# Probabilities and values in 32 bits in a banded attention and feed-forward kernel, with another order of issue

## The chip, the cores and the metric

The kernel runs on one core of one Trainium2 chip. The metric is the device time of one execution in microseconds (us); the time of a kernel is the median of its runs. A core has five engines that run side by side and meet at semaphores: TensorE (PE, whose weight loads are a row of their own, PEld), VectorE (DVE), ScalarE (ACT), GpSimd (POOL) and SyncE (SP, which issues the transfers). Each engine takes its instructions in the order in which the program lists them.

## What is computed

One layer of a transformer in 32 bit floats over 4 sequences of 2048 rows of 256: layer norm, attention in 16 heads of 16 in which each row sees itself and the 63 rows before it, a residual sum, layer norm, a feed-forward block with weights rounded to -1, 0 and 1, and a residual sum.

```python
x = x + attention(layernorm(x), Wq, Wk, Wv, Wo)
x = x + ffn(layernorm(x), W1, b1, W2, b2)

# attention
scores = einsum('bhqd,bhkd->bhqk', q, k) / sqrt(16) + bias   # bias: 0 where i-64 < j <= i, else -inf
attn = softmax(scores, axis=-1)
out = einsum('bhqk,bhkd->bhqd', attn, v)
return einsum('bsd,ed->bse', out.reshape(B, S, D), Wo)

# ffn
h = relu(einsum('bsd,fd->bsf', x, ternary(W1)) + b1)
return einsum('bsf,df->bsd', h, ternary(W2)) + b2
```

## The kernel before

The 8192 rows are cut into 32 chunks `c` of 256 rows, and a chunk into 4 blocks `b` of 64 query rows. A block of queries meets a window of 128 keys. TensorE multiplies 16 bit operands, so the kernel writes each 32 bit operand as a high and a low 16 bit part and adds two or three products of parts.

A chunk goes through these steps. `norm_in` normalises and splits the rows and transposes them by a transfer into `xT`. `project` makes q, k and v; for v (L627) the product in PSUM is cast into the high half of a tile `vo` by ACT (L643), the rest is subtracted into its low half by DVE (L645), and three transfers (L649, L651, L655) copy the rows into `ve`, the same values shifted by 64 rows, so that blocks of even number also find their window in one tile. A column of ones beside each pair's 32 value columns makes the sum of the probabilities fall out of the same product. `stack` puts parts of q and k over each other into `st`, so that one product does the work of three. `maxima` (L731) multiplies queries and keys for the row maximum, which DVE takes (L738) and a transfer writes back into `st`. `weights` (L771) multiplies again, now with the maximum subtracted inside the product, into a PSUM bank of 128 keys by 512 columns (8 heads of 64 queries, in two halves `g` per block).

The two steps that the change touches come next. `weights` takes the exponential of that bank and splits it. In the variant used for all 256 half blocks, ACT writes the exponential in 32 bits to a tile `r` (L781), casts it to the 16 bit `ph` (L784), and POOL subtracts to get `pl` (L786). `values` multiplies: for each of the 8 pairs of heads in a block, three products accumulate in one PSUM place, high by high (L812), high by the low part of the values (L813) and low by high (L814). In each, the probabilities, 128 keys by 128 queries of the two heads, are loaded into TensorE's array as weights, and 34 or 32 value columns are streamed past. DVE then takes the reciprocal of the sums (L827) and scales (L830) into `o`.

`wo_out` (L861) projects the result, `normalized` normalises it, and `ffn1` (L896) and `ffn2` (L936, L937) are the feed-forward block. `ffn1` also has two variants to split its result: ACT writes the high part (L915) and DVE subtracts (L917), or ACT writes 32 bits (L906), casts (L909) and POOL subtracts (L911).

The order of all this is not the order of the source. Each step is a generator that yields the engine it is about to use and a planned cost (`"P", 0.6` for a block of `values`). The class `Lanes` runs a plan with these costs: of the steps that could start soonest it takes the one with the lowest priority number, which is made from the chunk, `PRIO`, `SLOPE` and `EARLY`. What it takes is issued then, and `chain` ties each engine's instructions in that order. `Lanes.pick` chooses between the variants of a step by the load that the plan has put on each engine, weighted with `WT`. So a change of a planned cost or of these tables moves instructions of every kind, and can send a step to another engine. Rings of buffers (`BUFS`) limit how far steps run ahead: 6 PSUM banks in all, of which `values` holds at most 4 (`pv`), and 6 tiles or pairs of tiles of probabilities (`pp`).

Of the kernel before, what the change touches and what calls it, by code (L numbers as in the profile page):

```python
# [10 lines left out]
FP = mybir.dt.float32  # L11
HP = mybir.dt.float16
BF = mybir.dt.bfloat16
U8 = mybir.dt.uint8
AF = mybir.ActivationFunctionType
ALU = mybir.AluOpType
# [20 lines left out]
PARTS = slice(64, 112)  # L37
R = 113
BIGH = 60000.0
PRIO = {'norm': 22.87, 'proj': 45.21, 'max': -15.41, 'att': 28.99, 'val': -103.79, 'wo': -72.86, 'ffn': -195.42, 'ffn2': 67.42, 'mask': 69.79, 'prep': -8.89}  # L40
SLOPE = {'norm': 0.0, 'proj': 0.051, 'max': 0.158, 'att': 0.043, 'val': 0.156, 'wo': 0.0, 'ffn': -0.016, 'ffn2': 0.0, 'mask': 0.106, 'prep': -0.017}
BUFS = {'xt': 11, 'ln': 2, 'xT': 3, 'zT': 4, 'qk': 2, 'pp': 6, 'op': 2, 'o': 2, 'h': 7, 'r': 5, 'bank': 6, 'lin': 6, 'sp': 1, 'tp': 3, 'pv': 4}
BANKS = ("lin", "tp", "pv")
EARLY = {'norm': (0.0, 0.0, -1.01), 'proj': (0.0, 6.69, -1.97), 'max': (0.0, 0.0, 0.0), 'att': (0.0, -2.82, 0.0), 'val': (0.0, 6.48, 0.0), 'wo': (0.0, 0.0, -1.66), 'ffn': (0.0, 0.0, 0.0), 'ffn2': (0.69, 0.0, -3.29), 'mask': (0.0, 0.0, 0.0), 'prep': (0.0, -20.19, 0.0)}
TOL = 0.0
BOOST = 4.14
CHAIN = ('PE', 'DVE', 'Activation', 'Pool', 'SP')
LAT = {"P": 0.2, "A": 0.17, "D": 0.15, "G": 0.13, "S": 0.97}
TAU = 17.1
DMAF, DLAT = 1.06, 0.78  # L50
WINDOW = 3.4133
WT = {'P': 0.82, 'A': 1.13, 'D': 1.02, 'G': 0.94, 'S': 0.0}


class Lanes:
# [147 lines left out]
def kernel(ctx: ExitStack, tc: tile.TileContext, x, Wq, Wk, Wv, Wo, W1, b1, W2, b2, out):  # L203
# [32 lines left out]
    def get(name):  # L236
        return ("get", name)
# [37 lines left out]
    qcon = const.tile([128, C], HP, name="qcon")  # L275
    qone = const.tile([1, C], HP, name="qone")

    vot = [const.tile([128, 2, NT, NP, 34], HP, name=f"vo{i}") for i in range(NV)]
    vet = [const.tile([128, 2, NT, NP, 34], HP, name=f"ve{i}") for i in range(NV)]

    xts, xTs, vs, ps_, hs, wts = {}, {}, {}, {}, {}, {}

# [2 lines left out]
    def constants():  # L285
        yield "G", 0.4
        make_identity(nc, ident)
        yield "D", 0.605
        nc.vector.memset(mhalf, -0.5)
        nc.vector.memset(ones, 1.0)  # L290
        nc.vector.memset(shift, PSHIFT * 4.0)
        signal("const")
        yield "D", 0.3
        nc.vector.tensor_copy(identh, ident)
        signal("ident")
        for i in range(NV):
            yield "G", 0.9
            nc.gpsimd.memset(vot[i][:, :, :, :, 32:34], 0.0)
            nc.gpsimd.memset(vot[i][:, 0, :, :, 32:33], 1.0)
            nc.gpsimd.memset(vet[i][0:64, :, 0], 0.0)  # L300
            nc.gpsimd.memset(mht[i % NQ], 0.0)
            signal("vfree", i - NV)

# [35 lines left out]
    def loaded(src, key):  # L339
        yield get("xt")  # L340
        yield "S", (0.5, 0.9)
        wn = xpool.tile([128, 2, D], FP, name="xt")
        nc.sync.dma_start(out=wn, in_=src)
        wts[key] = wn
        signal("loaded", key)
# [266 lines left out]
    def project(c, nm):  # L612
        yield wait("weight", nm)
        yield wait("normed", c)
        xT = xTs[c]
        wh, wl = wts[nm]
        if nm == "v":
            yield wait("vfree", c - NV)
        yield get("lin")
        yield "P", 1.32  # L620
        ps = lin.tile([128, 2, C], FP, name="bank")
        if nm == "v":
            for t in range(NT):
                n = 0
                for d in range(2):
                    for i, b in ((0, wh), (1, wh), (0, wl)):
                        nc.tensor.matmul(ps[:, t, :], xT[:, i, d, t, :], b[:, d, :], start=n == 0, stop=n == 5)  # L627
                        n += 1
        else:
            for e in range(2):  # L630
                es = slice(e * 128, (e + 1) * 128)
                n = 0
                for d in range(2):
                    for a, i in ((wh, 0), (wh, 1), (wl, 0)):
                        nc.tensor.matmul(ps[:, e, :], a[:, d, es], xT[:, i, d], start=n == 0, stop=n == 5)  # L635
                        n += 1
        if tally(("proj", c), 3):
            put("xT")
        if nm == "v":
            vo, ve = vs[c] = vot[c % NV], vet[c % NV]  # L640
            psv = ps.rearrange("p u (a r) -> p u a r", r=32)
            yield "A", 0.485
            nc.scalar.copy(vo[:, 0, :, :, 0:32], psv)  # L643
            yield "D", 0.605
            nc.vector.tensor_tensor(vo[:, 1, :, :, 0:32], psv, vo[:, 0, :, :, 0:32], ALU.subtract)  # L645
            put("lin")
            signal("vo", c)
            yield "S", (0.6, 0.75)
            nc.sync.dma_start(out=ve[64:128], in_=vo[0:64])  # L649
            yield "S", (0.72, 0.4)  # L650
            nc.sync.dma_start(out=ve[0:64, :, 1:NT], in_=vo[64:128, :, 0:NT - 1])  # L651
            if c % NCB:
                yield wait("vo", c - 1)
                yield "S", (0.72, 0.4)
                nc.sync.dma_start(out=ve[0:64, :, 0], in_=vs[c - 1][0][64:128, :, NT - 1])  # L655
                if tally(("vdone", c - 1), 2):
                    signal("vfree", c - 1)
            if (c + 1) % NCB == 0 and tally(("vdone", c), 2):
                signal("vfree", c)
            signal("v", c)  # L660
            return
        if ("hl", c) not in ps_:
            ps_["hl", c] = None
            yield get("qk")
            ps_["hl", c] = qkp.tile([128, 2, 2, 2, C], HP, name="hl")
            signal("hl", c)
        yield wait("hl", c)
        hl = ps_["hl", c][:, "qk".index(nm)]
        yield "A", 0.485
        nc.scalar.copy(hl[:, 0], ps)  # L670
        yield "D", 0.605
        nc.vector.tensor_tensor(hl[:, 1], ps, hl[:, 0], ALU.subtract)
        put("lin")
        signal(nm, c)
# [88 lines left out]
    def weights(c, b, g):  # L763
        yield get("pp")
        yield get("tp")
        yield "P", 0.24
        tp = tps.tile([128, 8, W], FP, name="bank")
        for i in range(8):
            j = g * 8 + i
            h = place(j)  # L770
            nc.tensor.matmul(tp[:, i], window(c, h, b)[0:R + 1], st[c % NQ][0:R + 1, 0, h, b * W:b * W + W], start=True, stop=True)  # L771
        used(c)
        tpf = tp.rearrange("p h q -> p (h q)")
        ph = pp.tile([128, 4, 128], HP, name="ph")
        pl = pp.tile([128, 4, 128], HP, name="pl")
        phf, plf = (t.rearrange("p a b -> p (a b)") for t in (ph, pl))
        if lanes.pick([[("D", 0.605), ("A", 0.97)], [("G", 1.2), ("A", 1.005)]]):
            yield get("r")
            yield "A", 0.485
            pf = rp.tile([128, 512], FP, name="r")  # L780
            nc.scalar.activation(pf, tpf, AF.Exp, scale=0.25 / (SW * SW))  # L781
            put("tp")
            yield "A", 0.52
            nc.scalar.copy(phf, pf)  # L784
            yield "G", 1.2
            nc.gpsimd.tensor_tensor(plf, pf, phf, ALU.subtract)  # L786
            put("r")
        else:
            yield "A", 0.485
            nc.scalar.activation(tpf, tpf, AF.Exp, scale=0.25 / (SW * SW))  # L790
            yield "A", 0.485
            nc.scalar.copy(phf, tpf)
            yield "D", 0.605
            nc.vector.tensor_tensor(plf, tpf, phf, ALU.subtract)
            put("tp")
        ps_[c, b, g] = (ph, pl)
        signal("p", c, b, g)

    def values(c, b):
# [3 lines left out]
        vo, ve = vs[c]  # L803
        v = vo if b % 2 else ve
        yield get("pv")
        yield "P", 0.6
        pv = pvp.tile([128, NP, 34], FP, name="bank")
        for g in range(2):
            ph, pl = ps_.pop((c, b, g))
            for i in range(4):  # L810
                p = g * 4 + i
                nc.tensor.matmul(pv[:, p, :], ph[:, i, :], v[:, 0, b // 2, p, :], start=True, stop=False)  # L812
                nc.tensor.matmul(pv[:, p, 0:32], ph[:, i, :], v[:, 1, b // 2, p, 0:32], start=False, stop=False)  # L813
                nc.tensor.matmul(pv[:, p, :], pl[:, i, :], v[:, 0, b // 2, p, :], start=False, stop=True)  # L814
            put("pp")
        if tally(("val", c), NB) and tally(("vdone", c), 2):
            signal("vfree", c)
# [128 lines left out]
        put("xt")  # L946

    for i, gen in enumerate([constants(), load(0)]):
        lanes.add(-9 + i, gen)
    for i, (nm, src) in enumerate((("q", Wq), ("k", Wk), ("v", Wv))):  # L950
        lanes.add(-7 + i, loaded(src.rearrange("(c p) d -> p c d", p=128), nm))
        start("proj", 0, weight_qkv(nm), i - 5)
    for c in range(NCH):
        if c:
# [34 lines left out]
```

## Time and profile before

| | |
|---|---|
| median of 3 runs | 671.49 us (671.26 to 676.62) |
| the profiled execution | 671.55 us |
| span of its instructions on the core | 669.8 us |
| mean granted TensorE clock | 0.987 |
| PE busy | 93% |
| DVE, ACT, POOL busy | 83%, 79%, 83% |

The profile gives each engine's busy time, cuts the span into 40 slices with the busy share of each in tenths, follows back the chain that ended last, and lists the costliest groups of instructions: line, engine, operation, tile written and tiles read with their shapes, the count, then the busy time and the mean of one in ns, then the engine's idle time ahead of them and who ended it. A matmul's record runs from its start until its modelled end, and records of successive matmuls overlap: a group of 1024 matmuls of 177 ns does not fill 1024 x 177 ns. What a matmul costs the engine is read from the distance between the starts of successive records in the timeline.

### The profile page before, as it was taken

To read this page: it belongs to the slowest core of one execution; us is meant where nothing else is said; L and a number is where in the kernel's file an instruction comes from. 1 tells how busy PE (TensorE), PEld (TensorE's weight loads), DVE (VectorE), ACT (ScalarE), POOL (GpSimd) and SP (SyncE) were. 2 spreads that over 40 slices of the span, in tenths; PEclk is the share of its full clock that TensorE was granted. 3 is DMA by queue.
4 is the path that set the end of the run, shared out by engine and by line. 5 is a ranking of instruction groups with operands and counts; after the bars stand their busy time and mean duration, and the time that the engine had idled before them with its cause. 6 is when DMAs were issued, how large, how long until landed. Compare 5 with 4: busy or idle time off the path is not lost.

```text
span 669.8 us, 30496 instructions
## 1 busy us (share of the span) xinstructions
PE 626.2 (93%) x12892; PEld 548.3 (82%) x12892; DVE 556.4 (83%) x1195; ACT 529.1 (79%) x1074; POOL 558.5 (83%) x639
## 2 busy tenths in 40 slices
PE   2867889999999999999999999999999999999997
PEld 1646777888888888888888879898788888988986
DVE  6788989888987998898989898878878997897763
ACT  6966969877999689988879969686879589987741
POOL 5676989979899879998989979898789689998830
PEclk9977998999999999999999999999999999999999
DMA  6684465766777668865785665589555954542232
GB/s 180 167 154 107 82 130 115 120 129 109 138 132 127 133 115 132 146 115 142 143 140 127 131 96 141 119 142 145 90 124 126 156 122 106 116 107 60 49 81 62
DMA packets 165032, 81.34 MB, mean 121 GB/s; under 512 B 110880, under 2 KB 162848, under 8 KB 164896
## 3 DMA queue, kind: packets, MB, share of 16 engines
q1 hardware_dynamic: 164896, 79.39, 61.5%
q8 instruction: 101, 1.65, 1.2%
q14 instruction: 35, 0.29, 0.2%
HBM read 11.67 MB, written 8.39 MB: 30 GB/s over the span
## 4 chain that ended last, share of the span: by engine, by line
PE 56%; POOL 13%; DVE 11%; ACT 7%; DMA 6%; issue 5%; SPq 3%; POOLq 0%; DVEq 0%; ACTq 0%
PE bank L896 11%; PE bank L635 7%; POOL pl L786 7%; PE bank L771 6%; PE bank L936 6%; PE bank L937 5%; PE sp L731 5%; PE bank L861 5%; PE bank L627 3%; DMA xt<-in_dram 3%; PE bank L814 3%; PE bank L812 2%; PE bank L813 2%; DVE mx L738 2%; ACT ph L784 2%
## 5 line engine op out<-in xcount | busy, mean ns | idle before, releaser
L786 POOL TENSOR_TENSOR pl<-r,ph 128x512 f16<-128x512 f32 x256 | 304.5, 1210 | 17.3 <-ACT ph L784 10.9
L781 ACT ACTIVATE r<-bank 128x512 f32<-128x512 f32 x256 | 145.5, 599 | 32.2 <-PE bank L771 26.9
L784 ACT CAST ph<-r 128x512 f16<-128x512 f32 x256 | 151.0, 629 | 0.7
L738 DVE TENSOR_REDUCE mx<-sp 128x8 f32<-128x768 f32 x128 | 121.8, 952 | 14.7 <-PE sp L731 13.0
L896 PE MATMUL bank<-zT,wq 128*128 128x256 f16 x1024 | 125.5, 273 | 0.3 <-DVE hl L917 0.2
L936 PE MATMUL bank<-wq,hh 128*128 128x256 f16 x512 | 119.7, 273 | 0.0
L937 PE MATMUL bank<-wq,hl 128*128 128x256 f16 x512 | 119.2, 272 | 0.0
L917 DVE SCALAR_TENSOR_TENSOR hl<-bank,hh 128x512 f16<-128x512 f32 x126 | 85.2, 685 | 34.8 <-ACT hh L915 33.2
L896 PEld LDWEIGHTS <-wq 128*128 128x128 f16 x1024 | 97.8, 98 | 12.5 <-issue 0.3
L915 ACT ACTIVATE hh<-bank 128x512 f16<-128x512 f32 x126 | 75.4, 604 | 31.9 <-PE bank L896 31.7
L771 PE MATMUL bank<-st 114*128 114x64 f16 x2048 | 86.9, 194 | 3.8 <-DMA st<-mst 1.4
L812 PEld LDWEIGHTS <-ph 128*128 128x128 f16 x1024 | 82.3, 96 | 4.2 <-DVE o L830 1.8
L814 PEld LDWEIGHTS <-pl 128*128 128x128 f16 x1024 | 79.9, 96 | 5.0 <-POOL pl L786 4.4
L771 PEld LDWEIGHTS <-st 114*128 114x128 f16 x2048 | 74.5, 98 | 11.4 <-issue 2.8
L813 PEld LDWEIGHTS <-ph 128*128 128x128 f16 x1024 | 80.5, 96 | 1.8 <-issue 0.6
L830 DVE TENSOR_TENSOR o<-bank,rec 64x128 f32<-64x128 f32 x256 | 73.8, 288 | 8.4 <-POOL nb L570 0.5
L731 PE MATMUL sp<-st 113*32 113x96 f16 x4096 | 69.7, 211 | 9.5 <-DVE mx L738 4.8
L731 PEld LDWEIGHTS <-st 113*32 113x32 f16 x4096 | 51.3, 98 | 26.9 <-issue 23.9
L936 PEld LDWEIGHTS <-hh 128*128 128x128 f16 x512 | 49.8, 97 | 6.0
L937 PEld LDWEIGHTS <-hl 128*128 128x128 f16 x512 | 50.0, 98 | 4.7
L597 POOL TENSOR_TENSOR op<-o,op 128x512 f16<-128x512 f32 x32 | 39.2, 1225 | 16.6 <-ACT op L844 16.0
L526 DVE BATCH_NORM_STATS2 st<-xt 128x6 f32<-128x256 f32 x128 | 47.8, 415 | 6.0 <-DMA xt<-in_dram 5.0
(117 smaller groups left out, 1493.0 us busy)
## 6 DMA issues: line engine op xcount, KB each, us to landing
st<-hl SPq DMA_DIRECT2D x192, 128.0 KB, 4.1
xt<-in_dram SPq DMA_DIRECT2D x44, 256.0 KB, 4.1
out_dram<-xt SPq DMA_DIRECT2D x32, 256.0 KB, 2.7
ve<-vo SPq DMA_DIRECT2D x32, 136.0 KB, 2.6
ve<-vo SPq DMA_DIRECT2D x60, 68.0 KB, 3.3
oT<-op SPq DMA_TRANSPOSE x64, 3.2
xT<-ht SPq DMA_TRANSPOSE x32, 3.5
st<-mst SPq DMA_DIRECT2D x32, 8.0 KB, 2.2
```

Of the source, the lines that this page charges most:

```text
L731: nc.tensor.matmul(sp[32 * n:32 * n + 32, p, 0:96], st[c % NQ][0:R, 0, h, b * W + q * 32:b * W + q * 32 + 32], window(c, h, b)[0:R, 32 * q ...
L738: nc.vector.tensor_reduce(ps_["mx", c][:, u], sp[:, :, 0:96], AX.X, ALU.max)
L771: nc.tensor.matmul(tp[:, i], window(c, h, b)[0:R + 1], st[c % NQ][0:R + 1, 0, h, b * W:b * W + W], start=True, stop=True)
L781: nc.scalar.activation(pf, tpf, AF.Exp, scale=0.25 / (SW * SW))
L784: nc.scalar.copy(phf, pf)
L786: nc.gpsimd.tensor_tensor(plf, pf, phf, ALU.subtract)
L812: nc.tensor.matmul(pv[:, p, :], ph[:, i, :], v[:, 0, b // 2, p, :], start=True, stop=False)
L813: nc.tensor.matmul(pv[:, p, 0:32], ph[:, i, :], v[:, 1, b // 2, p, 0:32], start=False, stop=False)
L814: nc.tensor.matmul(pv[:, p, :], pl[:, i, :], v[:, 0, b // 2, p, :], start=False, stop=True)
L896: nc.tensor.matmul(ps[:, u], wq1[:, d + d * i, fs], zT[:, i, d], start=n == 0, stop=n == 3)
L936: nc.tensor.matmul(ps[:, t, :], hh[:, f % 2, ts], wq2[:, f, :], start=f == 0, stop=False)
L937: nc.tensor.matmul(ps[:, t, :], hl[:, f % 2, ts], wq2[:, f, :], start=False, stop=f == NF - 1)
```

## The change

The probabilities and the values stay in 32 bits. `weights` loses its two variants: ACT writes the exponential in 32 bits into a tile `p` that `values` reads directly; the casts and the subtractions are gone. `values` makes one product of 32 bit operands per pair of heads in place of three products of 16 bit parts, with 33 value columns. `vo` and `ve` hold 32 bit values and no low half; the values leave PSUM in one copy, on DVE or ACT as `pick` decides; the transfers from `vo` to `ve` stay, with rows of 33 x 4 bytes in place of two halves of 34 x 2. A constant `FIRST` shifts the first tasks of the program, and the tables of the planner have new numbers, among them the planned cost of a block of `values`, 0.5 in place of 0.6.

```diff
-PRIO = {'norm': 22.87, 'proj': 45.21, 'max': -15.41, 'att': 28.99, 'val': -103.79, 'wo': -72.86, 'ffn': -195.42, 'ffn2': 67.42, 'mask': 69.79, 'prep': -8.89}
+PRIO = {'norm': 20.14, 'proj': 55.77, 'max': -43.93, 'att': 22.72, 'val': -95.02, 'wo': -81.89, 'ffn': -208.09, 'ffn2': 85.49, 'mask': 80.83, 'prep': 0.99}
...
-TOL = 0.0
-BOOST = 4.14
+TOL = 0.06
+FIRST = -23.03
+BOOST = 3.17
...
-TAU = 17.1
-DMAF, DLAT = 1.06, 0.78
+TAU = 6.85
+DMAF, DLAT = 1.1, 0.95
...
-WT = {'P': 0.82, 'A': 1.13, 'D': 1.02, 'G': 0.94, 'S': 0.0}
+WT = {'P': 0.7, 'A': 1.13, 'D': 1.04, 'G': 0.7, 'S': 0.0}
...
-    vot = [const.tile([128, 2, NT, NP, 34], HP, name=f"vo{i}") for i in range(NV)]
-    vet = [const.tile([128, 2, NT, NP, 34], HP, name=f"ve{i}") for i in range(NV)]
+    vot = [const.tile([128, NT, NP, 33], FP, name=f"vo{i}") for i in range(NV)]
+    vet = [const.tile([128, NT, NP, 33], FP, name=f"ve{i}") for i in range(NV)]
...
-            yield "A", 0.485
-            nc.scalar.copy(vo[:, 0, :, :, 0:32], psv)
-            yield "D", 0.605
-            nc.vector.tensor_tensor(vo[:, 1, :, :, 0:32], psv, vo[:, 0, :, :, 0:32], ALU.subtract)
+            if lanes.pick([[("D", 0.605)], [("A", 0.485)]]):
+                yield "A", 0.485
+                nc.scalar.copy(vo[:, :, :, 0:32], psv)
+            else:
+                yield "D", 0.605
+                nc.vector.tensor_copy(vo[:, :, :, 0:32], psv)
...
-        ph = pp.tile([128, 4, 128], HP, name="ph")
-        pl = pp.tile([128, 4, 128], HP, name="pl")
-        phf, plf = (t.rearrange("p a b -> p (a b)") for t in (ph, pl))
-        if lanes.pick([[("D", 0.605), ("A", 0.97)], [("G", 1.2), ("A", 1.005)]]):
-            yield get("r")
-            yield "A", 0.485
-            pf = rp.tile([128, 512], FP, name="r")
-            nc.scalar.activation(pf, tpf, AF.Exp, scale=0.25 / (SW * SW))
-            put("tp")
-            yield "A", 0.52
-            nc.scalar.copy(phf, pf)
-            yield "G", 1.2
-            nc.gpsimd.tensor_tensor(plf, pf, phf, ALU.subtract)
-            put("r")
...
-        ps_[c, b, g] = (ph, pl)
+        p = pp.tile([128, 4, 128], FP, name="p")
+        yield "A", 0.485
+        nc.scalar.activation(p.rearrange("p a b -> p (a b)"), tpf, AF.Exp, scale=0.25 / (SW * SW))
+        put("tp")
+        ps_[c, b, g] = p
...
-        yield "P", 0.6
+        yield "P", 0.5
...
-            ph, pl = ps_.pop((c, b, g))
+            pr = ps_.pop((c, b, g))
             for i in range(4):
                 p = g * 4 + i
-                nc.tensor.matmul(pv[:, p, :], ph[:, i, :], v[:, 0, b // 2, p, :], start=True, stop=False)
-                nc.tensor.matmul(pv[:, p, 0:32], ph[:, i, :], v[:, 1, b // 2, p, 0:32], start=False, stop=False)
-                nc.tensor.matmul(pv[:, p, :], pl[:, i, :], v[:, 0, b // 2, p, :], start=False, stop=True)
+                nc.tensor.matmul(pv[:, p, 0:33], pr[:, i, :], v[:, b // 2, p, :], start=True, stop=True)
...
-        lanes.add(-9 + i, gen)
+        lanes.add(FIRST - 9 + i, gen)
...
-        lanes.add(-7 + i, loaded(src.rearrange("(c p) d -> p c d", p=128), nm))
+        lanes.add(FIRST - 7 + i, loaded(src.rearrange("(c p) d -> p c d", p=128), nm))
```

More of the change, by code (lines that the diff above doesn't have):

```diff
@@ L39 @@
 BIGH = 60000.0
-PRIO = {'norm': 22.87, 'proj': 45.21, 'max': -15.41, 'att': 28.99, 'val': -103.79, 'wo': -72.86, 'ffn': -195.42, 'ffn2': 67.42, 'mask': 69.79, 'prep': -8.89}
-SLOPE = {'norm': 0.0, 'proj': 0.051, 'max': 0.158, 'att': 0.043, 'val': 0.156, 'wo': 0.0, 'ffn': -0.016, 'ffn2': 0.0, 'mask': 0.106, 'prep': -0.017}
+PRIO = {'norm': 20.14, 'proj': 55.77, 'max': -43.93, 'att': 22.72, 'val': -95.02, 'wo': -81.89, 'ffn': -208.09, 'ffn2': 85.49, 'mask': 80.83, 'prep': 0.99}
+SLOPE = {'norm': 0.042, 'proj': 0.092, 'max': 0.2, 'att': -0.132, 'val': 0.112, 'wo': -0.076, 'ffn': 0.165, 'ffn2': 0.111, 'mask': 0.185, 'prep': 0.005}
 BUFS = {'xt': 11, 'ln': 2, 'xT': 3, 'zT': 4, 'qk': 2, 'pp': 6, 'op': 2, 'o': 2, 'h': 7, 'r': 5, 'bank': 6, 'lin': 6, 'sp': 1, 'tp': 3, 'pv': 4}
 BANKS = ("lin", "tp", "pv")
-EARLY = {'norm': (0.0, 0.0, -1.01), 'proj': (0.0, 6.69, -1.97), 'max': (0.0, 0.0, 0.0), 'att': (0.0, -2.82, 0.0), 'val': (0.0, 6.48, 0.0), 'wo': (0.0, 0.0, -1.66), 'ffn': (0.0, 0.0, 0.0), 'ffn2': (0.69, 0.0, -3.29), 'mask': (0.0, 0.0, 0.0), 'prep': (0.0, -20.19, 0.0)}
-TOL = 0.0
-BOOST = 4.14
+EARLY = {'norm': (-30.14, 24.57, 24.46), 'proj': (5.96, 26.39, 8.9), 'max': (22.36, -20.51, -17.0), 'att': (-17.56, -29.92, -22.98), 'val': (8.13, -16.32, 6.52), 'wo': (19.8, 5.25, 5.57), 'ffn': (25.59, -3.9, 4.92), 'ffn2': (-2.2, -11.62, -21.64), 'mask': (-16.08, 0.76, 4.5), 'prep': (-15.84, -4.17, 23.26)}
+TOL = 0.06
+FIRST = -23.03
+BOOST = 3.17
 CHAIN = ('PE', 'DVE', 'Activation', 'Pool', 'SP')
 LAT = {"P": 0.2, "A": 0.17, "D": 0.15, "G": 0.13, "S": 0.97}
-TAU = 17.1
-DMAF, DLAT = 1.06, 0.78
+TAU = 6.85
+DMAF, DLAT = 1.1, 0.95
 WINDOW = 3.4133
-WT = {'P': 0.82, 'A': 1.13, 'D': 1.02, 'G': 0.94, 'S': 0.0}
+WT = {'P': 0.7, 'A': 1.13, 'D': 1.04, 'G': 0.7, 'S': 0.0}
 class Lanes:
@@ L297, in constants @@
             yield "G", 0.9
-            nc.gpsimd.memset(vot[i][:, :, :, :, 32:34], 0.0)
-            nc.gpsimd.memset(vot[i][:, 0, :, :, 32:33], 1.0)
-            nc.gpsimd.memset(vet[i][0:64, :, 0], 0.0)
+            nc.gpsimd.memset(vot[i][:, :, :, 32:33], 1.0)
+            nc.gpsimd.memset(vet[i][0:64, 0], 0.0)
             nc.gpsimd.memset(mht[i % NQ], 0.0)
@@ L650, in project @@
             yield "S", (0.72, 0.4)
-            nc.sync.dma_start(out=ve[0:64, :, 1:NT], in_=vo[64:128, :, 0:NT - 1])
+            nc.sync.dma_start(out=ve[0:64, 1:NT], in_=vo[64:128, 0:NT - 1])
             if c % NCB:
@@ L654, in project @@
                 yield "S", (0.72, 0.4)
-                nc.sync.dma_start(out=ve[0:64, :, 0], in_=vs[c - 1][0][64:128, :, NT - 1])
+                nc.sync.dma_start(out=ve[0:64, 0], in_=vs[c - 1][0][64:128, NT - 1])
                 if tally(("vdone", c - 1), 2):
@@ L773, in weights @@
         tpf = tp.rearrange("p h q -> p (h q)")
-        ph = pp.tile([128, 4, 128], HP, name="ph")
-        pl = pp.tile([128, 4, 128], HP, name="pl")
-        phf, plf = (t.rearrange("p a b -> p (a b)") for t in (ph, pl))
-        if lanes.pick([[("D", 0.605), ("A", 0.97)], [("G", 1.2), ("A", 1.005)]]):
-            yield get("r")
-            yield "A", 0.485
-            pf = rp.tile([128, 512], FP, name="r")
-            nc.scalar.activation(pf, tpf, AF.Exp, scale=0.25 / (SW * SW))
-            put("tp")
-            yield "A", 0.52
-            nc.scalar.copy(phf, pf)
-            yield "G", 1.2
-            nc.gpsimd.tensor_tensor(plf, pf, phf, ALU.subtract)
-            put("r")
[L788 to L795, printed above, removed]
-        ps_[c, b, g] = (ph, pl)
+        p = pp.tile([128, 4, 128], FP, name="p")
[3 more added lines that the diff above has]
+        ps_[c, b, g] = p
         signal("p", c, b, g)
```

## The prediction

> **What bounds the kernel now.** I read the table of busy time first, then stages, then the groups by line, then the timeline of one block of `values`. The engines lie close together over the span, and the average doesn't say who is late.
>
> ```profile
> PE 626.2 (93%) x12892; PEld 548.3 (82%) x12892; DVE 556.4 (83%) x1195; ACT 529.1 (79%) x1074; POOL 558.5 (83%) x639
> ```
>
> The busy times of three stretches do (columns: stretch and its length, then busy us and instructions of PE, PEld, DVE, ACT and POOL, then the granted clock, the share of the transfers and GB/s):
>
> ```profile
> 0.00:110.00 110.00, 76.77 (x1519) 62.86 (x1520) 90.25 (x203) 85.99 (x180) 82.47 (x106) 0.93 0.64 137
> 110.00:640.00 530.00, 523.58 (x11140) 462.58 (x11139) 452.70 (x971) 434.44 (x879) 472.18 (x527) 1.00 0.65 121
> 640.00:670.00 30.00, 25.86 (x237) 22.90 (x235) 13.46 (x23) 8.64 (x15) 3.85 (x7) 1.00 0.24 70
> ```
>
> From 110 to 640 us PE is idle for 6.4 us of 530, at full clock; DVE, ACT and POOL have 58 to 96 us free there. Only the first 110 us have PE idle for 33 us. So each us of TensorE time added after 110 us is a us of the result, and work taken from ACT and POOL is worth at most the idle of PE that they cause.
>
> What they cause is small. In the groups, ACT and POOL spend much on the split, but the matmuls that follow hardly wait (ahead of the bar: busy and mean ns; behind: idle before, and its releaser):
>
> ```profile
> L786 POOL TENSOR_TENSOR pl<-r,ph 128x512 f16<-128x512 f32 x256 | 304.5, 1210 | 17.3 <-ACT ph L784 10.9
> L784 ACT CAST ph<-r 128x512 f16<-128x512 f32 x256 | 151.0, 629 | 0.7
> L814 PE MATMUL bank<-ve,pl 128*128 128x34 f16 x512 | 46.0, 178 | 2.2 <-POOL pl L786 2.0
> L937 PE MATMUL bank<-wq,hl 128*128 128x256 f16 x512 | 119.2, 272 | 0.0
> ```
>
> **What is removed from TensorE.** The timeline (start us, length us, engine, line) has the first and last matmuls of one block, 24 of them; the next block begins at 300.48:
>
> ```profile
> 299.88 0.18 PE L812 MATMUL bank<-vo,ph 128*128 128x34 f16 x1
> 299.91 0.18 PE L813 MATMUL bank<-vo,ph 128*128 128x32 f16 x1
> 299.93 0.18 PE L814 MATMUL bank<-vo,pl 128*128 128x34 f16 x1
> ...
> 300.48 0.18 PE L812 MATMUL bank<-ve,ph 128*128 128x34 f16 x1
> ```
>
> A block is 0.60 us, 25 ns per product although a load of 128 x 128 weights goes ahead of each. 128 blocks: 77 us removed. The records' 178 ns are latency that overlaps, and would have made it seven times as much.
>
> **What is added.** 8 products a block, 1024 in all, with 32 bit weights of 128 x 128 and 33 columns. The trace has two products of this form, the column sums in the preparation of the feed-forward weights (L455, 4 columns). The second stands in a dense stream at full clock (its neighbours are 0.11 us apart). Two answers on the loads, the first cut short by its window, then the matmuls:
>
> ```profile
> 28.21 0.19 PEld L455 LDWEIGHTS bank<-asum,ones 128*128 128x128 f32 x1
> 28.21 0.30 PEld L455 LDWEIGHTS bank<-asum,ones 128*128 128x128 f32 x2
> ...
> 28.21 0.27 PE L627 MATMUL bank<-wvl,xT 128*128 128x256 f16 x1
> 28.32 0.28 PE L455 MATMUL bank<-asum,ones 128*128 128x4 f32 x2
> 28.46 0.27 PE L635 MATMUL bank<-xT,wkh 128*128 128x256 f16 x1
> ```
>
> One product in the source is two passes here, each with its own load and matmul. A load lasts 0.19 us, where the 16 bit loads last 0.10, and the second starts 0.30 - 0.19 = 0.11 us after the first. The matmuls' records stand apart too: the first is 0.17 us by itself, the pair 0.28, so the second ends 0.11 later with only 4 columns to stream. The pass is paced by its load, at 110 ns. The whole product took only 28.46 - 28.32 = 0.14 us of the stream, because its first load ran under the 0.11 us of L627; in a block of eight products the neighbour is another such pass, and nothing long stands over the loads. I take 2 x 110 = 220 ns per product: 1024 x 0.22 = 225 us.
>
> The columns cost less than the load. Four 32 bit transposes (L371) take 1.06 us in the timeline with 0.42 for each record, so (1.06 - 0.42) / 3 = 213 ns apart for 128 columns, at a time when the neighbouring 256 column matmuls are 0.21 us apart, twice their later distance: that is half clock, and 107 ns or 0.83 ns a column at full. 33 columns are 28 ns a pass, and 16 bit matmuls show that streaming and the next load run side by side.
>
> The bounds of the price: 55 ns (two passes paced by their columns, loads free), 140 ns (one load of the two hidden, as at L455), 276 ns (load and columns one after the other, 2 x (110 + 28)). 220 is nearest to the row with this operation, in the only state the block can be in.
>
> The Trainium skill speaks against the change here: "TensorE: Matmul & The Clock Gate", Weight-path perf modes, has the fast load of 128 weights off for 32 bit operands; its section on LDWEIGHTS gives columns / 1.2 GHz, 107 ns, which would make an estimated 2 x 107 x 1024 = 219 us. "Perfetto Trace Analysis", Engine Utilization, speaks for it: a 32 bit matmul at half the array's output rate, an estimated 28 ns for 33 columns and 28 us in all; the L455 rows, 110 ns a pass with 4 columns, contradict that where weights change each time.
>
> **The other engines.** By the order of the changed program, 106 of the 128 `ffn1` splits go over ACT and POOL, not 2, and 12 more normalisations over ACT. ACT: 529 - 256 x 0.629 + 104 x 0.629 + 12 x 0.6 = 440 us. POOL: 558 - 256 x 1.21 + 104 x 1.21 + 3 = 377. DVE: 556 - 104 x 0.685 (L917) - 32 x 0.688 (L645) - 12 x 0.963 (L577) + 3 = 455. None comes near a span of 700 to 800, so the saved 100 to 180 us on each cost and bring nothing beyond PE's waits. The moved `ffn1` split is longer, one cast of 0.62 and a subtraction of 1.16 for one of 0.69, 1.09 us later; L937's idle of 0.0 says that `ffn2` has other PE work ahead of it, which hides this. Without that cover it would be 104 x 1.09 = 113 us. SP issues 530 transfers in both programs, those to `ve` (136 and 68 KB) 3% smaller. `values` holds PE's queue 1.2 us longer per block; all that is queued behind it are PE's own matmuls, and the engines that wait for them have the slack above. The change adds no wait.
>
> The new order can move the start: 33 us of PE idle in the first 110, from waits on ACT, DVE and POOL and on transfers. No row prices it. Bounds: 10 us either way, about what the two longest waits there, 4.3 us each on ACT and POOL, come to; I take nothing. Some ten blocks lie in that stretch, each 1.16 us longer, and partly fill idle; with the 3 to 4 us of waits on `pl` that vanish I take off 8.
>
> **Sum**, against the profiled execution's 671.55 us (span 669.8 and 1.75 around it; the median, 671.49, is the same): 671.55 - 77 + 225 - 8 = 812 us, for this case 795 to 830.
>
> **Rivals.**
> Faster: 32 bit loads hide in a block as 16 bit ones do, and the 33 columns pace it. 55 ns x 1024 = 56 us, so 671.55 - 77 + 56 - 8 = 643 us. It decides if a product costs under (77 + 8) / 1024 = 83 ns. For it: the second record of the L455 pair starts early, about 30 ns after the first (28.32 to 28.46 is 0.14, less 0.11). Against: it ends 0.11 later.
> One load hidden: 140 ns, 143 us, 730 us. For it: it is what L455 took in the stream; against: its cover was a 256 column matmul.
> Load and columns in series: 276 ns, 283 us, 870 us. For it: two passes may need the array empty between them; 4 columns can't show it. Against: the 16 bit block.
> Half clock: loads leave the array with 28 ns of columns in 110. This trace halves the clock after a thin stretch, PE busy for 0.97 us of 4:
>
> ```profile
> 32.00:36.00 4.00, 0.97 (x8) 0.45 (x8) 3.79 (x5) 4.00 (x6) 4.00 (x5) 1.00 0.32 70
> 36.00:40.00 4.00, 2.21 (x42) 1.68 (x43) 2.39 (x4) 4.00 (x5) 3.23 (x3) 0.54 0.81 173
> ```
>
> In the changed order 92 blocks stand alone among denser products and 18 times two stand together, 3.5 us. If each pair costs as much again, +63, 875 us. Whether loads count as activity no row tells.
>
> **How the numbers follow.** First case 0.70, faster 0.09, one load hidden 0.06, in series 0.08, half clock 0.07. The range must take in the first case, with 10 us of start to spare, and reach to the series case and most of the half clock: 785 to 876, which leaves out the two cheaper cases and the edges, some 0.2. A change under 1%, 7 us, can't be told from none; only a product of about 75 to 90 ns would give it: 0.01. Faster 0.09, slower 0.90.
>
> **What would show it.** A group of 2048 loads of 128x128 f32 at about 0.19 us and a block of `values` of 1.76 us in the timeline; PE busy at 94% or more with DVE, ACT and POOL near 455, 440 and 377 us; granted clock still near 0.99; waits on `pl` gone and none in their place. A block of 0.5 us would make the forecast wrong on the load, one of 2.2 us on the overlap; a right block with another total would put the error in the order of issue.

## The result and the profile after

The changed kernel takes 848.32 us, the median of 4 runs from 835.96 to 859.04, against 671.6 us. The ratio is 1.248, 95% interval 1.234 to 1.262; it leaves out the two runs with the lowest clock, which is why it lies under the ratio of the medians. The profiled execution is the slowest of the four, 859.04 us with a span of 857.2 and a mean clock of 0.907; the others had 0.915 to 0.936.

The table of busy time and, from the 40 slices, PE's busy tenths and its granted clock:

```profile
PE 828.6 (97%) x11868; PEld 740.4 (86%) x11868; DVE 456.7 (53%) x1051; ACT 471.8 (55%) x930; POOL 381.7 (45%) x496
...
PE   4599999999999999999999999999999999999997
...
PEclk9677589998999999999969999998996899979999
```

DVE, ACT and POOL gave up 100, 57 and 177 us of work, and PE took 202 more; it is now the only engine near its limit. The clock row is new: dips of six to eight stand all along the span, where the kernel before has them only at the start. The first two stretches as before, and a third from there to 780 us, show both things (PE, PEld, DVE, ACT, POOL, clock, transfers):

```profile
0.00:110.00 110.00, 85.98 (x1044) 72.65 (x1045) 67.71 (x166) 62.37 (x130) 48.32 (x73) 0.75 0.52 120
110.00:640.00 530.00, 529.72 (x8052) 476.47 (x8051) 288.49 (x659) 304.25 (x600) 249.50 (x316) 0.94 0.54 98
640.00:780.00 140.00, 140.00 (x1909) 125.05 (x1909) 65.42 (x157) 69.78 (x136) 57.02 (x71) 0.85 0.41 82
```

From 110 to 640 us PE has 0.3 us of idle left in 530, and a clock of 0.94 in place of 1.00, then 0.85 until 780 us; after that it is 0.98. The chain of waits by engine, and what PE waited for (us in total, times, longest), say the same:

```profile
PE 90%; POOL 3%; ACT 3%; DMA 2%; DVE 1%; issue 1%; SPq 0%; POOLq 0%; DVEq 0%
```

```profile
PE bank L371 <- ACT r L360: 11.6, 5, 7.0
...
PE sp L733 <- DVE mx L740: 1.1, 3, 0.6
PE bank L796 <- ACT p L778: 0.5, 2, 0.3
```

PE carries 90% of the chain, where it was 56%. What it still waits for belongs to the weights' preparation (L371 above all); the new product waits for its probabilities for 0.5 us in all, so nothing took the place of the waits on `pl`. The groups of the new product, and one lone block of `values` in the timeline with its neighbours:

```profile
L796 PEld LDWEIGHTS bank<-vo,p 128*128 128x128 f32 x1024 | 133.7, 211 | 1.3 <-issue 0.2
L796 PE MATMUL bank<-ve,p 128*128 128x33 f32 x1024 | 134.1, 289 | 0.5 <-ACT p L778 0.5
```

```profile
301.63 0.27 PE L635 MATMUL bank<-xT,wkl 128*128 128x256 f16 x1
301.74 1.87 PE L796 MATMUL bank<-vo,p 128*128 128x33 f32 x16
303.44 0.22 PE L752 MATMUL bank<-identh,mh 128*128 128x128 f16 x1
```

Each of the two groups counts 1024, for two tiles: 2048 loads and 2048 matmuls for 1024 products, two passes each. A block runs from 301.74 to 303.44, 1.70 us where the three 16 bit products took 0.60. The median distance of two passes, worked out from the starts in the trace, is 112 ns at full clock and 213 ns at half.

### The profile page after: what moved, and what is told of

The parts are those of the page before. It is cut to its first block, busy times and chain, and to the rows that moved or that the text cites. A ratio compares the mean times of both kernels' runs of the same rounds, so it can differ in the third digit from the quotient of the medians.

```text
span 857.2 us, 27805 instructions
## 1 busy us (share of the span) xinstructions
PE 828.6 (97%) x11868; PEld 740.4 (86%) x11868; DVE 456.7 (53%) x1051; ACT 471.8 (55%) x930; POOL 381.7 (45%) x496
## 4 chain that ended last, share of the span: by engine, by line
PE 90%; POOL 3%; ACT 3%; DMA 2%; DVE 1%; issue 1%; SPq 0%; POOLq 0%; DVEq 0%
PE bank L796 29%; PE bank L878 13%; PE bank L635 9%; PE bank L773 8%; PE bank L918 7%; PE bank L919 7%; PE sp L733 7%; PE bank L627 5%; PE bank L843 5%; DMA xt<-in_dram 1%; POOL r L471 1%; POOL rs L531 1%; ACT st L333 0%; ACT r L449 0%; POOL ht L548 0%
## 5 line engine op out<-in xcount | busy, mean ns | idle before, releaser
L778 ACT ACTIVATE p<-bank 128x512 f32<-128x512 f32 x256 | 139.9, 597 | 127.3 <-PE bank L773 126.8
L893 POOL TENSOR_TENSOR hl<-r,hh 128x512 f16<-128x512 f32 x106 | 125.8, 1196 | 98.0 <-ACT hh L891 78.1
L809 DVE RECIPROCAL rec<-bank 128x8 f32<-128x8 f32 x128 | 26.5, 207 | 234.2 <-PE bank L796 234.2
L796 PE MATMUL bank<-vo,p 128*128 128x33 f32 x1024 | 136.4, 291 | 0.0
L796 PEld LDWEIGHTS bank<-vo,p 128*128 128x128 f32 x1024 | 133.7, 211 | 1.3 <-issue 0.2
L796 PE MATMUL bank<-ve,p 128*128 128x33 f32 x1024 | 134.1, 289 | 0.5 <-ACT p L778 0.5
L796 PEld LDWEIGHTS bank<-ve,p 128*128 128x128 f32 x1024 | 132.1, 209 | 2.4 <-ACT p L778 0.9
L888 ACT ACTIVATE r<-bank 128x512 f32<-128x512 f32 x106 | 63.1, 595 | 75.4 <-PE bank L878 75.3
L583 POOL TENSOR_TENSOR ht<-r,ht 128x512 f16<-128x512 f32 x32 | 37.7, 1179 | 65.4 <-ACT ht L579 65.4
L891 ACT CAST hh<-r 128x512 f16<-128x512 f32 x106 | 64.8, 618 | 1.9
```

What stands on the lines that cost most here:

```text
L778: nc.scalar.activation(p.rearrange("p a b -> p (a b)"), tpf, AF.Exp, scale=0.25 / (SW * SW))
L796: nc.tensor.matmul(pv[:, p, 0:33], pr[:, i, :], v[:, b // 2, p, :], start=True, stop=True)
L891: nc.scalar.copy(hh, r)
L893: nc.gpsimd.tensor_tensor(hl, r, hh, ALU.subtract)
```

## The experiments

The theory: a 32 bit pass is paced by loading its 128 weight columns, and the thin stream of 33 columns in 112 ns lets the granted clock fall to half (the expectations call what grants it the clock gate). Rivals: the columns or a fixed cost pace it; the order of issue carries part of the loss; the wrong planned cost of a block does.

**Order and bits apart.** The three 16 bit products with the changed kernel's tables (`PRIO`, `SLOPE`, `EARLY`, `FIRST`, `WT` and the rest), and the 32 bit product with the tables of before.

```diff
# order_alone, against before.py: the tables of after.py, and
...
-        lanes.add(-9 + i, gen)
+        lanes.add(FIRST - 9 + i, gen)
...
# bits_alone, against after.py: the tables of before.py, and
...
-        lanes.add(FIRST - 9 + i, gen)
+        lanes.add(-9 + i, gen)
...
```

> The split of before (three 16 bit products) with the changed kernel's tables of the planner. Theory (the 32 bit product is the cause, the order is nearly neutral): 660 to 685 us, within 2% of before. Rival (the new order is a large part of the loss): over 700 us. The order helps and hides part of the product's loss: under 655 us.

> The 32 bit product with the tables of before. Theory: like the changed kernel, 830 to 865 us, a pass of the product 112 ns, clock 0.90 to 0.94. Rival (the order carries the loss): under 760 us. If the new order is what thins the stream and halves the clock: clock over 0.96 and about 790 us.

The bits alone gave 838.42 us, ratio 1.239 (1.230 to 1.248): the loss is there without the new order, and the interval overlaps that of the changed kernel. Its clock, 0.937 to 0.964 in its four runs, lies for the most part above the 0.90 to 0.94 that was expected and above the changed kernel's 0.907 to 0.936: the half clock comes with the product, and the new order adds to it. The order alone gave 701.59 us, ratio 1.045 (1.042 to 1.047), a miss: I had expected it neutral. Its stretches beside those of before (on record in the prediction):

```profile
0.00:110.00 110.00, 76.80 (x1418) 62.18 (x1419) 82.81 (x190) 84.43 (x175) 78.16 (x103) 0.89 0.64 132
110.00:640.00 530.00, 513.83 (x10927) 451.50 (x10924) 444.53 (x933) 424.68 (x860) 463.95 (x508) 1.00 0.67 120
640.00:700.00 60.00, 45.36 (x561) 37.65 (x556) 28.53 (x63) 26.83 (x52) 33.31 (x40) 0.90 0.22 51
```

PE idles for 16.2 us between 110 and 640 us where it idled for 6.4, and from 640 to the end at 697.9 it idles for 12.5 in place of 3.9; the start has no more idle, but a lower clock. That is 18 of the 28 us of longer span; the rest is PE busy for longer, 636.0 us in place of 626.2. So under the 16 bit split, with DVE, ACT and POOL near 80%, the new order costs some 30 us. Whether that comes from the variants that `WT` and `TAU` choose or from the order, one more run tells:

```diff
# order_oldwt, against order_alone
-TAU = 6.85
+TAU = 17.1
-WT = {'P': 0.7, 'A': 1.13, 'D': 1.04, 'G': 0.7, 'S': 0.0}
+WT = {'P': 0.82, 'A': 1.13, 'D': 1.02, 'G': 0.94, 'S': 0.0}
```

> The 16 bit split with the new tables, but WT and TAU, which choose variants, as before. If the 30 us of the order alone come from the variants that it chooses (POOL's load counted at 0.70 in place of 0.94): back to 665 to 685 us. If they come from the order itself: 690 to 710 us.

699.01 us, ratio 1.039 (1.036 to 1.042): the choice of variants is worth a few us at most, the order the rest. The choices are nearly those of before in this run (POOL subtracts for 254 of the 256 half blocks, DVE for all 128 splits of `ffn1`), and the loss stays. Which entry of the order does it stays open.

**What paces a pass, and what the clock counts.** Three edits of the product, with the order of issue kept: 17 columns, 64 columns, and 64 of the 128 weight columns. The first and the last leave part of the results out, and DVE reads what is there for both heads of a pair.

```diff
# cols17
-                nc.tensor.matmul(pv[:, p, 0:33], pr[:, i, :], v[:, b // 2, p, :], start=True, stop=True)
+                nc.tensor.matmul(pv[:, p, 16:33], pr[:, i, :], v[:, b // 2, p, 16:33], start=True, stop=True)
...
# cols64
-        pv = pvp.tile([128, NP, 34], FP, name="bank")
+        pv = pvp.tile([128, NP, 64], FP, name="bank")
...
-                nc.tensor.matmul(pv[:, p, 0:33], pr[:, i, :], v[:, b // 2, p, :], start=True, stop=True)
+                n = 64 if p < NP - 1 else 33
+                nc.tensor.matmul(pv[:, p, 0:n], pr[:, i, :], v[:, b // 2].rearrange("x a r -> x (a r)")[:, p * 33:p * 33 + n], start=True, stop=True)
...
# w64
-                nc.tensor.matmul(pv[:, p, 0:33], pr[:, i, :], v[:, b // 2, p, :], start=True, stop=True)
+                nc.tensor.matmul(pv[0:64, p, 0:33], pr[:, i, 0:64], v[:, b // 2, p, :], start=True, stop=True)
...
```

> 17 of the 33 columns are streamed; the 16 value columns of each pair's first head are left out and those of the second used for both. Theory of the load: a pass stays at 110 to 112 ns. Rival, the columns pace it: a pass falls by 13 to 14 ns (16 columns x 0.83) and the kernel by 27 us. If the clock gate counts streamed columns, a thinner stream loses more clock: 0.88 to 0.91 and 850 to 880 us; if it counts loads too, no change.

> 64 columns are streamed for 7 of 8 products (the added ones go to unused columns of the bank and nothing reads them). Theory of the load with streaming beside it: a pass stays at 112 ns, since 64 columns are 53 ns. Rival, load and columns in series: 26 ns more a pass, +46 us. If the clock gate counts streamed columns, twice the columns keep the clock up: 0.96 or more, and the kernel is faster with more work, 785 to 815 us. If it doesn't: clock as before this edit, 835 to 860 us.

> Each product loads 64 of the 128 weight columns, so the second head of each pair is left out and DVE writes the first head's result twice. Theory (the pass is paced by its load, by the number of weight columns): a pass of 55 to 60 ns at full clock, a block of about 0.9 us, 105 to 120 us less than the changed kernel at equal clock: 700 to 745 us. Rival (a fixed cost of a 32 bit pass, or the streamed columns): a pass stays near 112 ns and the time within 2% of the changed kernel's.

17 columns took 884.58 us (882.38 to 894.72 in five runs), ratio 1.316 (1.312 to 1.319), and 64 columns 801.57 us (800.80 to 802.03 in four), ratio 1.194 (1.191 to 1.196); the four runs with 33 lie between, 835.96 to 859.04. Half the columns are slower and twice the columns faster. In both the median distance of two passes at full clock is 112 ns, as with 33 columns, so columns up to 64 cost nothing and do not pace it. What moves is the clock (span and mean clock, 17 columns first, then 64):

```profile
core 0: 892.8 us, clock 0.869
```

```profile
core 0: 799.6 us, clock 0.978
```

What is streamed holds the clock up, and loading, the same in all three, doesn't do so by itself: the products differ in nothing but columns that cost no time. The time at half clock is 2 x (1 - clock) x span: 234, 159 (the changed kernel) and 35 us, and the spans fall by 36 and 58 us with it, 0.47 us for each us at half clock. At full clock throughout, all three come to 799.6 - 0.47 x 35 = 783 us of span, and so do all 13 runs, within 782 to 785, though those of the changed kernel range from 107 to 159 us at half clock.

The trace also shows when the clock falls (counted from its clock intervals, which are multiples of 3.4 us, and from the starts of the passes). Between 110 us and the last 5 us the changed kernel's clock halves 16 times, and each time 21 to 30 passes start in the 3.4 us ahead, where a lone block has 16. Of the 171 other stretches of 3.4 us at full clock, 12 have 20 passes or more. With 64 columns 32 of 200 stretches have as many, and the clock falls in none. So the clock falls where two blocks of few columns lie close together; no run changes their spacing alone.

Half the weight columns gave 715.27 us, ratio 1.063 (1.059 to 1.067), in the expected range. In the timeline, two blocks in sequence:

```profile
409.53 1.12 PE L796 MATMUL bank<-vo,p 128*64 128x33 f32 x16
410.49 1.10 PE L796 MATMUL bank<-ve,p 128*64 128x33 f32 x16
```

16 passes in 0.96 us; the median distance is 58 ns, against 112 for 128 columns of weights. The load's width paces the pass. At full clock this kernel comes to an estimated 701 us of span, 82 below the 783, where 105 to 120 were expected at equal clock. The lone blocks account for that: from its start to the next matmul's one takes 1.05 us, not the 0.93 of 16 passes, against 1.71 in the changed kernel (medians of 89 and 72 blocks at full clock), and 128 x 0.66 is 84 us.

With 16 bits a product with 128 weight columns takes 25 ns of the stream. What the prediction cites from the Trainium skill, "TensorE: Matmul & The Clock Gate", Weight-path perf modes, the fast load off for 32 bit operands, agrees with 112 ns against 25. The halved array rate from "Perfetto Trace Analysis", Engine Utilization, 28 ns for a product by the prediction's estimate, is not what two passes of 112 ns cost where the weights change each time.

**Does a load hide under a long neighbour?** `values` takes matmuls of a waiting `ffn2` and issues one ahead of each product; then the same with 64 columns.

```diff
# mixed, in values (ffn2 puts its 32 matmuls on the list `dense` and issues what is left itself)
-        yield "P", 0.5
+        yield "P", 1.78
...
+                if dense:
+                    dense[0].pop(0)()
...
                 nc.tensor.matmul(pv[:, p, 0:33], pr[:, i, :], v[:, b // 2, p, :], start=True, stop=True)
# mixed64: as mixed, with the product of cols64
```

> Where an ffn2 is ready, one of its 256 column matmuls is issued ahead of each 32 bit product (ahead of 683 of the 1024 in the order, where 81 have such a neighbour in the changed kernel); the plan is told 1.78 us for a block. Theory (the first of the two loads hides under a long neighbour, as at L455): the pair of passes costs 140 ns there and not 220, 602 x 0.08 = 48 us less, and the denser stream keeps the clock up, together 755 to 800 us. Rival (a 32 bit load hides under nothing): only the clock gains, not below 790, with 220 ns from the first pass to the next matmul's start beyond the neighbour's 109.

> As the mixed one, with 64 streamed columns for 7 of 8 products. Theory: the two gains overlap, since both raise the clock; 48 us from hidden loads beside the 64 column version's 802: 740 to 765 us, clock 0.98 or more. Rival: loads hide under nothing: 795 to 805.

778.38 us, ratio 1.158 (1.152 to 1.163), in the expected range. Products and neighbours alternate in its timeline:

```profile
299.85 0.28 PE L921 MATMUL bank<-wq,hl 128*128 128x256 f16 x1
299.97 0.30 PE L801 MATMUL bank<-vo,p 128*128 128x33 f32 x2
300.11 0.28 PE L921 MATMUL bank<-wq,hh 128*128 128x256 f16 x1
300.23 0.30 PE L801 MATMUL bank<-vo,p 128*128 128x33 f32 x2
```

From a product's start to its neighbour's is 0.14 us, as at L455 in the kernel before: the first load of two lies under the neighbour (the median of 648 such products is 141 ns). The two gains can be told apart: at full clock throughout the four runs come to 745 us of span in place of 783, so some 38 us go with the hidden loads, where 48 were expected, and the rest of the gain is clock. With 64 columns 740 to 765 us were expected, and that is a miss: 773.81 us, ratio 1.153 (1.147 to 1.158), nothing that the intervals tell apart from the version with 33:

```profile
299.93 0.33 PE L802 MATMUL bank<-ve,p 128*128 128x64 f32 x2
300.10 0.27 PE L922 MATMUL bank<-wq,hl 128*128 128x256 f16 x1
300.21 0.31 PE L802 MATMUL bank<-ve,p 128*128 128x33 f32 x2
300.35 0.27 PE L922 MATMUL bank<-wq,hh 128*128 128x256 f16 x1
```

A product of 64 columns takes 0.17 us there, one of 33 columns 0.14. Where the load is hidden the added columns are paid: 606 products of 64 columns stand behind such a neighbour, an estimated 606 x 0.03 = 18 us, and at full clock the span is 758 us in place of 745. That takes back what the clock gives (0.975 to 0.986 in the runs, against 0.954 to 0.965).

**The plan, and the order once more.**

```diff
# plan_true, against after.py
-        yield "P", 0.5
+        yield "P", 1.78
# bits64: bits_alone with the product of cols64
```

> The changed kernel with the planned cost of a block of values at 1.78 us in place of 0.5; nothing else. Theory (PE is the bound and its stream has hardly a gap, so a truer plan has nothing to win but the clock): 830 to 865 us. Rival (the wrong planned cost makes waits): under 815 us.

> The 32 bit product with the tables of before, and 64 streamed columns for 7 of 8 products so that the clock is up and steady: beside the 64 column version with the new tables (802 us) it shows the order of issue alone. If the new order is neutral under the 32 bit product: 794 to 810 us. If it helps there as it hurts the 16 bit split (4.4%): 820 us or more. If it hurts in both: under 785 us.

The true planned cost changed nothing that can be told, 844.24 us, ratio 1.253 (1.247 to 1.259). With 64 columns and the old tables, 808.27 us, ratio 1.202 (1.199 to 1.206), against 1.191 to 1.196 with the new ones: under the 32 bit product the new order gains a little under 1% there. At full clock it is worth more, 14 us: by the same 0.47 us, both versions with the old tables come to some 797 us of span, those with the new ones to 783. With 33 columns the half clock that the new order adds (107 to 159 us in its runs, 59 to 107 without it) takes this back, 848.32 against 838.42 us.

No version here reaches the 671.6 us of the kernel before.

## Why the prediction was right, point by point

The forecast was 812 us in a range from 785 to 876; 848 lies in it, on the side that was forecast. The price of the new product, the largest term, was right for the reason given; that the total came this near is in part luck, since two errors of opposite sign partly cancelled.

The bound: right. PE was the limit, work taken off the other engines freed 57 to 177 us on each and brought only PE's waits. PE's idle fell from 669.8 - 626.2 = 43.6 us to 857.2 - 828.6 = 28.6, 15 us where 8 were taken off. The 64 column versions say why: PE idles for 809.6 - 770.0 = 39.6 us with the tables of before and 799.6 - 771.5 = 28.1 with the new ones, so some 4 us come with the product and 11 with the new order, which the sum had at nothing.

The price of a 32 bit product: right, and shown. The single product at L455 carried it, and the step that mattered was to set aside its 0.14 us in the stream and take the 110 ns between its loads twice. Measured, a pass is 112 ns and a block 1.70 us, not 1.76, because the first load of a block lies under its neighbour: 128 x 1.70 = 218 us for the 225. The rivals with 55, 140 and 276 ns fell: 64 columns cost no more than 17, which also shows columns and the next load side by side. The 0.83 ns a column, read from the transposes of L371, was not shown by them: they are 213 ns apart at half clock, and so are the passes with 33 columns, so that distance can be the load's. 140 ns is real, but only with a dense neighbour ahead of each product.

At full clock the sum holds to within 20 us: 783 us against the span of before at full clock, an estimated 669.8 - 0.47 x 17 = 662, is 121 more, where -77 + 225 - 8 = 140 was written. From the measured terms it is -77 + 218 - 15 = 126.

The half clock is where the forecast fell short. It stood as a rival at 0.07, priced at 63 us, and not as a term of the sum; a clock still near 0.99 was one of the signs named, and it was 0.907 to 0.936. Half clock was there in every run of the changed kernel, 107 to 159 us of it, an estimated 0.47 x (107 - 17) = 42 to 0.47 x (159 - 17) = 67 us more than before. The two errors, 20 us too much in the sum and some 55 of clock too little in the typical run (848 - 785 at full clock, less 8 that the kernel before loses too), partly cancelled. The step that failed is "whether loads count as activity no row tells", after which the half clock was treated as unlikely; with the same loads and other columns the clock moved, so loads by themselves did not hold it up. The rival's trigger, blocks in sequence, agrees with the trace. The 2.8% between the runs of this kernel has the same cause: at full clock they come to 782 to 785 us.

The other engines: DVE 456.7 and POOL 381.7 us against 455 and 377, right; ACT 471.8 against 440, 32 too low. The lengths of ACT's records fell from 625.5 to 532.1 us, by 93 where the forecast took off 89; but records overlap, by 96 us before and by 60 after, and the forecast took lengths off a busy time in which they are merged. The longer `ffn1` split stayed covered: no wait of PE on it is in the list of waits. The new order, taken as nothing with bounds of 10 us, was worth some 14 us at full clock, beyond those bounds, and lost it again to the half clock; under the 16 bit split it costs 30 us, but that is not this change.

## What to carry to other kernels

Before merging several 16 bit products into one of 32 bits, count weight loads, not products: where each product brings its own 128 columns of weights and streams few, a 32 bit product here cost two passes of 112 ns, each paced by its load, against 25 ns for each of three 16 bit products. Look for one instruction of the new form anywhere in the old trace, preparation included, and read the distance of its passes, not its share of a stream that hides half of it. Then ask how much is streamed per us: a stream of loads with few columns can be busy in every record and still run at half clock, and a block interleaved with dense matmuls gains twice, some 38 us here from the hidden loads and the rest from the clock.

## What the runs showed that I had not expected

More streamed columns made the kernel faster: 17, 33 and 64 columns gave 884.58, 848.32 and 801.57 us at 112 ns a pass throughout, with mean clocks of 0.869, 0.907 and 0.978 in their profiles (0.907 to 0.936 over the runs with 33). And one set of tables for the order costs 4.5% under one split of the work, and under the other gains a little under 1% where the clock holds and nothing that can be told where it doesn't.
